# Selective scan on one core: products with C for both channel halves in one GpSimd instruction, in place, and their sums two groups later

## The chip, the core and the metric

The kernel runs on one core of one Trainium2 chip. The metric is the device time of one execution in microseconds; the median of three runs of the kernel before is 34,734.67 us (34,729.47 to 34,738.2). Engines are named as in the profile: PE is TensorE, DVE is VectorE, ACT is ScalarE, POOL is GpSimd, SP issues DMA transfers.

## The reference

Four layers follow each other on an image of 256 x 256 positions with 128 channels. The change touches layer 1 alone, a selective scan in four directions over 256 inner channels with 16 states each:

```python
def selective_scan(xs, dts, As, Bs, Cs, Ds, dt_bias):
    delta = jax.nn.softplus(dts + dt_bias[None, :, :, None])
    ...
    def step(h, inp):
        d_t, x_t, B_t, C_t = inp
        dA = jnp.exp(d_t[..., None] * As)
        h = dA * h + (d_t * x_t)[..., None] * B_t[:, :, None, :]
        y = jnp.einsum('bkdn,bkn->bkd', h, C_t)
        return (h, y)
    ...
    return ys + Ds[None, :, :, None] * xs
```

For every direction k, channel d, state n and position t: h = exp(delta * A) * h + delta * x * B, and y is the sum over the 16 states of h * C. B and C are the same for all channels. Everything is in 32-bit floats.

## The kernel before

The scan stage is the function `scan_stream`. Its four directions are walked one after the other, each in 128 chunks of 512 positions (CH), in all N = 512 chunks. The 256 channels are two halves (dh = 0, 1) of 128 partitions. A chunk is worked in NG = 8 groups, called s = 0 to 7 in its loop: group j handles half j % 2 and the four states that begin at j // 2 * 4. So groups 0 and 1 are the two halves of the same four states and use the same four rows of B and of C; two such groups are called a pair here, numbered 0 to 3 in the chunk.

Each group takes these steps, on four engines:

- `b_product` (L736): the term delta * x * B of 4 states x 512 positions (128 x 2048), on GpSimd for groups 2, 4 and 6, on VectorE for the other five. The table `b_order` says at which s each of them is issued.
- `scans` (L769): two scans of 128 x 1024 on VectorE, each over two states laid end to end. For each, ScalarE first writes the decay exp(delta * A) into one of two PSUM tiles (`l1b_da`, L754, two instructions of 512) and repairs the seam between the two states (L758). The result is `l1b_h`, 4 states x 512.
- `keep_state` (L780): ScalarE copies the last column of h as the start for the next chunk. It is issued in the next group, after the first scan.
- `c_product` (L784): GpSimd multiplies h by C, 128 x 2048, into a tile of its own, `l1b_hc`.
- `sums` (L803): TensorE adds the four states of the product into one of two PSUM tiles `l1b_y`, by four matmuls with the identity. The first group of each half starts the sum with the skip term (L791 or L793, `y_start`). Sums of group g - 2 are issued in group g.
- `y_out` (L813): ScalarE copies the finished sum of a chunk into the output block, at s = 1 and s = 2 of the next chunk.

Between these stands the preparation of the next chunk on TensorE and ScalarE: `dt` (L675) writes delta before its softplus into the PSUM tile `l1b_mm`, `soft_abs` and `soft_exp` (L687 to L695) form the parts of the softplus, `soft_sum` (L701) adds them on TensorE, `delta_copy` (L709) takes the result, `delta_x` (L717, VectorE) multiplies it by x in PSUM, and for half 0 `du_copy` (L725, ScalarE, at s = 4) copies that product to SBUF for GpSimd. `dt` of half 1 comes after it, since it overwrites the same tile. `xproj` (L643, at s = 5) computes dt, B and C of the chunk after next.

The order on each engine is the order in which the Python code issues the instructions (`manual_schedule`); only the waits are derived from the tiles. A tile pool with `bufs=3` gives three buffers in turn: the first write to the fourth tile waits until the last use of the first has ended. `l1b_h` and `l1b_hc` have three buffers of 128 x 2048 each. B and C arrive as broadcasts of 1 MB per pair (`load_b`, L663; `load_c`, L669), three buffers each, issued by SP in the code's order, behind the last use of the buffer that they fill.

Of the kernel before, what the change touches and what calls it, by code (L numbers as in the profile page):

```python
# [10 lines left out]
F32 = mybir.dt.float32  # L11
AF = mybir.ActivationFunctionType
ALU = mybir.AluOpType
# [4 lines left out]
P = 128  # L18
S = 256
NPOS = S * S  # L20
CH = 512
# [530 lines left out]
def scan_stream(c, xc2, y, w):  # L552
# [7 lines left out]
    tc, nc = c.tc, c.nc  # L560
    G, BL, NG = 4, 1024, 8
# [8 lines left out]
    N = len(chunks)  # L570
    with ExitStack() as a:
# [3 lines left out]
        wk = a.enter_context(tc.tile_pool(name="l1b_wk", bufs=2))  # L575
        dram = a.enter_context(tc.tile_pool(name="l1b_dr", bufs=4, space=DRAM))
        ps1 = a.enter_context(tc.tile_pool(name="l1b_p1", bufs=1, space=PSUM))
        states = [st.tile([P, 2, 16], F32, name=f"l1b_state{k}") for k in range(4)]
# [6 lines left out]
        ys = [ps1.tile([P, CH], F32, name=f"l1b_y{dh}") for dh in range(2)]  # L585
# [2 lines left out]

        mm = ps1.tile([P, CH], F32, name="l1b_mm")
        du1 = ps1.tile([P, CH], F32, name="l1b_du")  # L590
        blocks, bcs, bbs, ccs, soft, dls, dbs, hs, hcs = ({} for _ in range(9))

        def cols(ch):
            return bass.ds(chunks[ch][1] * CH % BL, CH)
# [1 line left out]
        def in_block(yo, ch, dh):  # L596

            k, i = chunks[ch]
            if k % 2 == 0:
                return yo[:, dh, cols(ch)]  # L600
            v = yo[:, dh].rearrange("p (b w r) -> p w b r", w=NW, r=R)
            return v[:, bass.ds(i * CH % BL // S, CH // S)]
# [62 lines left out]
        def load_c(m):  # L665
            if m < 4 * N:
                n0 = 16 + m % 4 * G
                cc = ccs[m] = bcp.tile([P, G, CH], F32, name="l1b_cc")
                nc.sync.dma_start(cc, bcs[m // 4][n0 : n0 + G][None].to_broadcast([P, G, CH]))  # L669
# [13 lines left out]
        def soft_abs(ch):  # L683
            if ch >= N:
                return
            soft[ch] = [wk.tile([P, CH], F32, name=f"l1b_{n}", bufs=1) for n in ("tail", "relu")]
            nc.scalar.activation(soft[ch][0], mm, AF.Abs)  # L687
            nc.scalar.activation(soft[ch][1], mm, AF.Relu)

        def soft_exp(ch):  # L690
            if ch >= N:
                return
            tail = soft[ch][0]
            nc.scalar.activation(tail, tail, AF.Exp, scale=-1.0)
            nc.scalar.activation(tail, tail, AF.Ln, bias=1.0)  # L695
# [7 lines left out]
        def delta_copy(ch, dh):  # L703

            if ch >= N:
                return
            k = chunks[ch][0]
            dl = dls[ch, dh] = wk.tile([P, CH], F32, name=f"l1b_dl{dh}")
            nc.scalar.copy(dl, mm)  # L709
            af = dls[ch, dh, "first"] = wk.tile([P, 16], F32, name=f"l1b_af{dh}")  # L710
            t0 = CH - 1 if k >= 2 else 0
            nc.scalar.activation(af, w["A"][:, k, dh], AF.Exp, scale=dl[:, t0 : t0 + 1])
# [8 lines left out]
        def du_copy(ch):  # L721
            if ch >= N:
                return
            dls[ch, "du"] = wk.tile([P, CH], F32, name="l1b_dus")
            nc.scalar.copy(dls[ch, "du"], mm)  # L725
# [12 lines left out]
        def scans(g, extras):  # L738
            ch, j = divmod(g, NG)
            k, dh, n0, rev = chunks[ch][0], j % 2, j // 2 * G, chunks[ch][0] >= 2  # L740
            db = dbs.pop(g).rearrange("p g t -> p (g t)")
            h = hs[g] = wk.tile([P, G, CH], F32, name="l1b_h", bufs=3)
            hf = h.rearrange("p g t -> p (g t)")
            dl, af = dls[ch, dh], dls[ch, dh, "first"]
            mid = CH - 1 if rev else CH
            for i in range(2):
                one, two = n0 + 2 * i + rev, n0 + 2 * i + 1 - rev
                da = das[i].rearrange("p g t -> p (g t)")
                if g == 0 or ch == N // 2 and j == 0:
                    nc.vector.memset(da[:, mid : mid + 1], 0.0)  # L750
                for n in (one, two):
                    o = n % 2 * CH
                    lo, hi = (0, CH) if n == one else (0, CH - 1) if rev else (1, CH)
                    nc.scalar.activation(  # L754
                        da[:, o + lo : o + hi], dl[:, lo:hi], AF.Exp, scale=w["A"][:, k, dh, n : n + 1]
                    )
                first = db[:, 2 * i * CH + mid : 2 * i * CH + mid + 1]
                nc.scalar.activation(  # L758
                    first,
                    states[k][:, dh, two : two + 1],  # L760
                    AF.Identity,
                    scale=af[:, two : two + 1],
                    bias=first,
                )
                sl = slice(2 * i * CH, 2 * i * CH + 2 * CH)
                h_, a_, d_ = hf[:, sl], da, db[:, sl]
                if rev:
                    h_, a_, d_ = h_[:, ::-1], a_[:, ::-1], d_[:, ::-1]
                nc.vector.tensor_tensor_scan(  # L769
                    h_, a_, d_, states[k][:, dh, one : one + 1], ALU.mult, ALU.add  # L770
                )
                if i == 0 and g:
                    keep_state(g - 1)
                for extra in extras[i]:
                    extra()

        def keep_state(g):
            ch, j = divmod(g, NG)
            k, dh, n0 = chunks[ch][0], j % 2, j // 2 * G
            nc.scalar.copy(states[k][:, dh, n0 : n0 + G], hs[g][:, :, 0 if k >= 2 else CH - 1])  # L780

        def c_product(g):
            hc = hcs[g] = wk.tile([P, G, CH], F32, name="l1b_hc", bufs=3)
            nc.gpsimd.tensor_tensor(hc, hs[g], ccs[g // 2], ALU.mult)  # L784
            hs.pop(g - 1, None)

        def y_start(ch, dh):
            k = chunks[ch][0]
# [8 lines left out]
        def sums(g):  # L797
            ch, j = divmod(g, NG)
            if j < 2:
                y_start(ch, j)  # L800
            hc = hcs.pop(g)
            for i in range(G):
                nc.tensor.matmul(  # L803
                    ys[j % 2], c.ident, hc[:, i], start=False, stop=j // 2 * G + i == 15
                )

        def y_out(ch, dh):
            if ch < 0:
                return
            k, i = chunks[ch]  # L810
            yo = blocks[ch][1]
            got = ys[dh] if k % 2 == 0 else ys[dh].rearrange("p (w b r) -> p w b r", b=S // R, r=R)
            nc.scalar.copy(in_block(yo, ch, dh), got)  # L813
            if dh == 1 and ch % 2 == 1:
                block_dma(k, i, yo, True)
# [23 lines left out]
        for ch in range(N):  # L839
            nxt = ch + 1  # L840
            for s in range(NG):
                g = NG * ch + s
                if s == 3 and ch % 2 == 0:
                    load_y(ch + 2)
                if s == 5 and ch % 2 == 1:
                    load_x(ch + 3)
                if s == 4:
                    delta_x(nxt, 0)
                for j in b_order.get(s, ()):
                    b_product(NG * ch + j)  # L850
                extras = [[], []]
                if s == 1:
                    extras[1] = [lambda: soft_abs(nxt), lambda: y_out(ch - 1, 0)]
                if s == 2:
                    extras = [[lambda: soft_exp(nxt)], [lambda: y_out(ch - 1, 1)]]
                if s == 3:
                    extras[1] = [lambda: delta_copy(nxt, 0)]
                if s == 4:
                    extras[0] = [lambda: du_copy(nxt)]
                if s == 5:  # L860
                    extras = [[lambda: soft_abs(nxt)], [lambda: soft_exp(nxt)]]
                if s == 6:
                    extras[1] = [lambda: xd_copy(ch + 2)]
                if s == 7:
                    extras[0] = [lambda: delta_x(nxt, 1), lambda: b_product(g + 2)]
                    extras[1] = [lambda: delta_copy(nxt, 1)]
                if s == 0:
                    dt(nxt, 0)
                scans(g, extras)
                if s == 2:  # L870
                    soft_sum(nxt)
                if s == 4:
                    dt(nxt, 1)
                if s == 5:
                    xproj(ch + 2)
                if s == 6:
                    soft_sum(nxt)
                if g >= 2:
                    sums(g - 2)
                c_product(g)  # L880
                if s % 2 == 1:
                    load_b(g // 2 + 4)
                    load_c(g // 2 + 3)
        keep = N * NG
        sums(keep - 2)
        y_out(N - 1, 0)
        sums(keep - 1)
        y_out(N - 1, 1)


def scan_weights(c, pool):
# [791 lines left out]
```

## Time and profile before

| Part of the profile before | Value |
|---|---|
| Median time | 34,734.67 us |
| Span of the profiled run | 34,733.3 us |
| Mean granted TensorE clock | 0.914 |
| C products (L784), GpSimd | 18,456.6 us in 4096 instructions |
| B products (L736), GpSimd | 6974.1 us in 1536 instructions |
| B products (L736), VectorE, all three rows | 4656.4 us in 2048 instructions, and 1170.8 us in 512 |
| Sums (L803), TensorE | 16,057.6 us in 32,768 records, 639 ns each |
| State copies (L780), ScalarE | 789.3 us in 4095 instructions |
| Copies of delta * x (L725), ScalarE | 300.2 us in 512 instructions, waiting for L736 |

How it is read: a row of the groups gives the busy time of all instructions of one line and shape, the mean of one, and then how long the engine stood idle right before them and which instruction ended that idleness. An idle stretch matters only on an engine whose lateness others feel. The page averages over all layers, so questions on the scan stage are put to stretches of time inside it, and to the timeline, which lists the instructions in order: start, length (of a run of equal instructions together), engine, line, operation, tiles, the number of instructions, and in brackets the idle time ahead with what ended it. One matmul of the code stands as two records.

### The profile page before, as it was taken

The numbers are of one execution on the slowest core, as the hardware profiler recorded it, in microseconds if no ns is written. First come the engines' busy times: TensorE is split into PE (matmuls) and PEld (weight loads), VectorE is DVE, ScalarE is ACT, GpSimd is POOL, SyncE is SP. The second block draws the span as 40 slices with busy tenths as digits, with TensorE's granted clock in tenths as the row PEclk, the third lists the DMA queues.
The fourth block names the chain that finished last, engine by engine and source line by source line (L and its number), as shares of the span: only waits on it lengthen the run. The fifth ranks groups of instructions, "written<-read, shape, count | busy, mean of one in ns | idle before, by whom it ended". The sixth has DMA issues, their size and how long they took to land. (4 is left out here: it accounts for less than half of the span.)

```text
span 34733.3 us, 255526 instructions
## 1 busy us (share of the span) xinstructions
PE 29234.8 (84%) x72564; PEld 12237.5 (35%) x72564; DVE 31351.6 (90%) x24081; ACT 22504.7 (65%) x46445; POOL 26723.0 (77%) x6476
## 2 busy tenths in 40 slices
PE   7999888888888888888888888888888888878888
PEld 2554333333333333333333333333333333334444
DVE  5668899999999999999999999999999999852699
ACT  3665577777777777777777777777777777432476
POOL 2441199999999999999999999999999999510000
PEclk8999999999999999999999999999999999989888
DMA  3114655555555555555555555555555555674111
GB/s 135 45 45 103 155 190 191 190 191 191 189 192 189 191 191 190 191 190 191 197 200 203 200 201 202 200 201 202 200 203 202 200 202 200 217 197 139 67 34 33
DMA packets 2561382, 5947.79 MB, mean 171 GB/s; under 512 B 899079, under 2 KB 1835800, under 8 KB 1984086
## 3 DMA queue, kind: packets, MB, share of 16 engines
q1 hardware_dynamic: 2424790, 5864.31, 47.3%
q10 hardware_dynamic: 135168, 67.13, 0.6%
q8 instruction: 572, 9.37, 0.1%
q14 instruction: 852, 6.98, 0.1%
HBM read 5238.41 MB, written 692.58 MB: 171 GB/s over the span
## 5 line engine op out<-in xcount | busy, mean ns | idle before, releaser
L769 DVE TENSOR_TENSOR_SCAN l1b_h<-l1b_da,l1b_state,l1b_db 128x1024 f32<-128x1024 f32 x8192 | 18788.8, 2335 | 597.7 <-ACT l1b_db L758 586.6
L784 POOL TENSOR_TENSOR l1b_hc<-l1b_h,l1b_cc 128x2048 f32<-128x2048 f32 x4096 | 18456.6, 4533 | 322.5 <-DVE l1b_h L769 321.7
L803 PE MATMUL l1b_y<-l1b_hc,ident 128*128 128x512 f32 x32768 | 16057.6, 639 | 1124.1 <-POOL l1b_hc L784 1124.0
L754 ACT ACTIVATE l1b_da<-l1b_dl,l_A 128x512 f32<-128x512 f32 (+1 forms) x16384 | 11296.7, 689 | 3153.2 <-DVE l1b_h L769 2845.3
L803 PEld LDWEIGHTS l1b_y<-l1b_hc,ident 128*128 128x128 f32 x32768 | 6526.7, 205 | 10695.3 <-issue 8153.0
L736 POOL TENSOR_TENSOR l1b_db<-l1b_bb,l1b_dus 128x2048 f32<-128x2048 f32 x1536 | 6974.1, 4540 | 1244.8 <-DMA l1b_bb<-l1b_bc 1244.8
L736 DVE TENSOR_TENSOR l1b_db<-l1b_bb,l1b_du 128x2048 f32<-128x2048 f32 x2048 | 4656.4, 2274 | 35.1
L758 ACT ACTIVATE l1b_db<-l1b_state,l1b_db,l1b_af 128x1 f32<-128x1 f32 x8192 | 3045.1, 372 | 0.0
L675 PE MATMUL l1b_mm<-l1b_xd,l_dtw 41*128 41x512 f32 x2048 | 1370.9, 754 | 1698.9 <-ACT l1b_dus L725 1693.2
L701 PE MATMUL l1b_mm<-l1b_tail,ident 128*128 128x512 f32 x2048 | 1295.4, 719 | 1384.3 <-ACT l1b_tail L695 1384.3
L780 ACT COPY l1b_state<-l1b_h 128x4 f32<-128x4 f32 x4095 | 789.3, 193 | 2433.0 <-DVE l1b_h L769 2432.9
L326 POOL TENSOR_TENSOR l0b_e<-l0b_e,l0b_den 128x1024 f32<-128x1024 f32 x512 | 970.0, 1895 | 1402.3 <-DVE l0b_den L325 784.0
L701 PE MATMUL l1b_mm<-l1b_relu,ident 128*128 128x512 f32 x2048 | 1310.3, 728 | 0.0
L675 PEld LDWEIGHTS l1b_mm<-l1b_xd,l_dtw 41*128 41x128 f32 x2048 | 337.3, 206 | 2513.3 <-ACT l1b_dus L725 2116.2
L725 ACT COPY l1b_dus<-l1b_mm 128x512 f32<-128x512 f32 x512 | 300.2, 586 | 1387.5 <-DVE l1b_db L736 1387.0
L736 DVE TENSOR_TENSOR l1b_db<-l1b_bb,l1b_mm 128x2048 f32<-128x2048 f32 x512 | 1170.8, 2287 | 18.2 <-ACT l1b_dus L725 0.7
L302 DVE CUSTOM_DVE_ANT_0 l0b_e<-l0b_sc,l0b_bias 128x256 f32<-128x256 f32 x2048 | 745.5, 421 | 419.3 <-PE l0b_sc L291 415.9
L701 PEld LDWEIGHTS l1b_mm<-l1b_tail,ident 128*128 128x128 f32 x2048 | 377.6, 207 | 2055.0 <-ACT l1b_tail L695 1810.6
L493 DVE SCALAR_TENSOR_TENSOR l1a_mm<-l1a_xi,l1a_each,l1a_mm 128x512 f32<-128x512 f32 x1408 | 1046.0, 755 | 59.0 <-issue 12.9
L643 PE MATMUL l1b_du<-l1b_xc,l_xproj 128*40 128x512 f32 x2048 | 981.5, 602 | 62.5 <-DMA l_xproj<-in_l_xproj 58.6
L317 ACT ACTIVATE l0b_e<-l0b_e,l0b_top 128x256 f32<-128x256 f32 x2048 | 1012.0, 498 | 1.9 <-DVE l0b_top L302 1.9
L709 ACT COPY l1b_dl<-l1b_mm 128x512 f32<-128x512 f32 x1024 | 588.3, 574 | 524.1 <-DVE l1b_du L717 516.6
(256 smaller groups left out, 28736.5 us busy)
## 6 DMA issues: line engine op xcount, KB each, us to landing
l1b_bb<-l1b_bc SPq DMA_DIRECT2D x2048, 1024.0 KB
l1b_cc<-l1b_bc SPq DMA_DIRECT2D x2048, 1024.0 KB
l1b_xc<-l_xc SPq DMA_DIRECT2D x128, 1024.0 KB
l_y<-l1b_yo SPq DMA_DIRECT2D x128, 1024.0 KB
l1b_xc<-l_xct SPq DMA_DIRECT2D x128, 1024.0 KB
l_y<-l1b_yo SPq DMA_DIRECT2D x256, 512.0 KB
l_xc<-l1a_o SPq DMA_DIRECT2D x64, 1024.0 KB
l_xct<-l1a_ot SPq DMA_DIRECT2D x16, 4096.0 KB
```

What stands on the lines that cost most here:

```text
L317: nc.scalar.activation(e[:, i], e[:, i], AF.Exp, scale=-1.0, bias=top[:, i : i + 1], accum_out=den[:, i : i + 1],)
L326: nc.gpsimd.tensor_tensor(e, e, den[:, :, None].to_broadcast([P, 4, S]), ALU.mult)
L493: nc.vector.scalar_tensor_tensor(mm, xis[i][:, r + dy : r + dy + 2, dx : dx + S], each[:, dh, tap : tap + 1], mm, ALU.mult, ALU.add,)
L643: nc.tensor.matmul(du1[:40], w["xproj"][:, dh, k, :], blocks[ch][0][:, dh, cols(ch)], start=dh == 0, stop=dh == 1,)
L675: nc.tensor.matmul(mm, w["dt"][:, chunks[ch][0], dh * P : dh * P + P], xds[ch % 3][0:41], start=True, stop=True,)
L701: nc.tensor.matmul(mm, c.ident, part, start=i == 0, stop=i == 1)
L736: eng.tensor_tensor(db, bbs[g // 2], du[:, None, :].to_broadcast([P, G, CH]), ALU.mult)
L754: nc.scalar.activation(da[:, o + lo : o + hi], dl[:, lo:hi], AF.Exp, scale=w["A"][:, k, dh, n : n + 1])
L758: nc.scalar.activation(first, states[k][:, dh, two : two + 1], AF.Identity, scale=af[:, two : two + 1], bias=first,)
L769: nc.vector.tensor_tensor_scan(h_, a_, d_, states[k][:, dh, one : one + 1], ALU.mult, ALU.add)
L784: nc.gpsimd.tensor_tensor(hc, hs[g], ccs[g // 2], ALU.mult)
L803: nc.tensor.matmul(ys[j % 2], c.ident, hc[:, i], start=False, stop=j // 2 * G + i == 15)
```

## The change

The two halves of a pair now share one tile `l1b_h` of 2 x 4 x 512 per partition, in three buffers, and `l1b_hc` is gone. The scans write the halves; once both are scanned, a single GpSimd instruction of 4096 elements per partition multiplies the whole tile by C in place, C being broadcast over the halves. It is issued after the scans of the following group, at even s. The sums read `l1b_h` and come in group g for group g - 4 instead of g - 2, so that `y_out` moves from s = 1 and 2 to s = 3 and 4, and the `y_start` that opens a chunk's sums moves from s = 2 and 3 to s = 4 and 5. The loads of C and of the x and y blocks move to fit. The aim is fewer GpSimd instructions and hand-overs, in the same amount of memory.

```diff
@@ scans
-            h = hs[g] = wk.tile([P, G, CH], F32, name="l1b_h", bufs=3)
-            hf = h.rearrange("p g t -> p (g t)")
+            if j % 2 == 0:
+                hs[g // 2] = wk.tile([P, 2, G, CH], F32, name="l1b_h", bufs=3)
+            hf = hs[g // 2][:, j % 2].rearrange("p g t -> p (g t)")
@@ keep_state, c_product
-            nc.scalar.copy(states[k][:, dh, n0 : n0 + G], hs[g][:, :, 0 if k >= 2 else CH - 1])
-
-        def c_product(g):
-            hc = hcs[g] = wk.tile([P, G, CH], F32, name="l1b_hc", bufs=3)
-            nc.gpsimd.tensor_tensor(hc, hs[g], ccs[g // 2], ALU.mult)
-            hs.pop(g - 1, None)
+            last = 0 if k >= 2 else CH - 1
+            nc.scalar.copy(states[k][:, dh, n0 : n0 + G], hs[g // 2][:, j % 2, :, last])
+
+        def c_product(m):
+
+            h = hs[m]
+            nc.gpsimd.tensor_tensor(h, h, ccs[m][:, None].to_broadcast([P, 2, G, CH]), ALU.mult)
@@ sums
-            hc = hcs.pop(g)
             for i in range(G):
                 nc.tensor.matmul(
-                    ys[j % 2], c.ident, hc[:, i], start=False, stop=j // 2 * G + i == 15
+                    ys[j % 2], c.ident, hs[g // 2][:, j % 2, i], start=False, stop=j // 2 * G + i == 15
                 )
+            if j % 2:
+                del hs[g // 2]
@@ the loop over chunks and groups
-                if s == 3 and ch % 2 == 0:
+                if s == 5 and ch % 2 == 0:
                     load_y(ch + 2)
-                if s == 5 and ch % 2 == 1:
+                if s == 6 and ch % 2 == 1:
                     load_x(ch + 3)
...
                 if s == 1:
-                    extras[1] = [lambda: soft_abs(nxt), lambda: y_out(ch - 1, 0)]
+                    extras[1] = [lambda: soft_abs(nxt)]
                 if s == 2:
-                    extras = [[lambda: soft_exp(nxt)], [lambda: y_out(ch - 1, 1)]]
+                    extras[0] = [lambda: soft_exp(nxt)]
                 if s == 3:
-                    extras[1] = [lambda: delta_copy(nxt, 0)]
+                    extras[1] = [lambda: delta_copy(nxt, 0), lambda: y_out(ch - 1, 0)]
                 if s == 4:
-                    extras[0] = [lambda: du_copy(nxt)]
+                    extras = [[lambda: du_copy(nxt)], [lambda: y_out(ch - 1, 1)]]
...
-                if g >= 2:
-                    sums(g - 2)
-                c_product(g)
+                if g >= 4:
+                    sums(g - 4)
+                if s % 2 == 0 and g >= 2:
+                    c_product(g // 2 - 1)
+                    load_c(g // 2 + 2)
                 if s % 2 == 1:
                     load_b(g // 2 + 4)
-                    load_c(g // 2 + 3)
```

After the last chunk the last product, four sums and two output copies follow.

More of the change, by code (lines that the diff above doesn't have):

```diff
@@ L590, in scan_stream @@
         du1 = ps1.tile([P, CH], F32, name="l1b_du")
-        blocks, bcs, bbs, ccs, soft, dls, dbs, hs, hcs = ({} for _ in range(9))
+        blocks, bcs, bbs, ccs, soft, dls, dbs, hs = ({} for _ in range(8))
         def cols(ch):
@@ L877, in scan_stream @@
                     soft_sum(nxt)
-                if g >= 2:
-                    sums(g - 2)
-                c_product(g)
+                if g >= 4:
[3 more added lines that the diff above has]
+                    load_c(g // 2 + 2)
                 if s % 2 == 1:
                     load_b(g // 2 + 4)
-                    load_c(g // 2 + 3)
[L884 to L888, printed above, removed]
+        c_product(N * NG // 2 - 1)
+        for j in range(4):
+            sums(N * NG - 4 + j)
+        for dh in range(2):
+            y_out(N - 1, dh)
 def scan_weights(c, pool):
```

## The prediction

> **What bounds the kernel now.** I read the page first (engine shares, then the costliest groups), then the groups of a window of 1000 us, then the timeline of a single chunk.
>
> ```profile
> PE 29234.8 (84%) x72564; PEld 12237.5 (35%) x72564; DVE 31351.6 (90%) x24081; ACT 22504.7 (65%) x46445; POOL 26723.0 (77%) x6476
> ...
> L769 DVE TENSOR_TENSOR_SCAN l1b_h<-l1b_da,l1b_state,l1b_db 128x1024 f32<-128x1024 f32 x8192 | 18788.8, 2335 | 597.7 <-ACT l1b_db L758 586.6
> L784 POOL TENSOR_TENSOR l1b_hc<-l1b_h,l1b_cc 128x2048 f32<-128x2048 f32 x4096 | 18456.6, 4533 | 322.5 <-DVE l1b_h L769 321.7
> ```
>
> The scan stage runs 512 chunks of 8 groups: 8192 scans are 16 per chunk, 4096 products with C are 8. In a window of 1000 us inside it VectorE is busy 974.9 us and GpSimd 987.8, and windows in all four scan directions agree within 0.4%. So both engines are nearly full. The waits say which one drives: VectorE waits for ScalarE (L758), GpSimd waits for VectorE's scans (L769). VectorE together with a short ScalarE burst is the pace. Its idle time is 597.7 / 512 = 1.17 us per chunk, all that a removed wait could give back.
>
> One chunk in the timeline (s is the group within the chunk). VectorE:
>
> ```profile
> 15038.83 2.29 DVE L736 TENSOR_TENSOR l1b_db<-l1b_bb,l1b_mm 128x2048 f32<-128x2048 f32 x1
> 15041.03 6.95 DVE L769 TENSOR_TENSOR_SCAN l1b_h<-l1b_da,l1b_state,l1b_db 128x1024 f32<-128x1024 f32 x3
> 15048.61 2.35 DVE L769 TENSOR_TENSOR_SCAN l1b_h<-l1b_da,l1b_state,l1b_db 128x1024 f32<-128x1024 f32 x1 [0.62 <-ACT l1b_db L758]
> 15051.47 6.83 DVE L769 TENSOR_TENSOR_SCAN l1b_h<-l1b_da,l1b_state,l1b_db 128x1024 f32<-128x1024 f32 x3 [0.52 <-ACT l1b_db L758]
> ```
>
> The two idle stretches (0.62 and 0.52 us) are the whole loss of the chunk; the second scan of s=5 stands at 15048.61, the first scan of s=6 at 15051.47. The same start came at 15001.53 one chunk earlier: the period is 49.94 us. ScalarE and TensorE in the same stretch:
>
> ```profile
> 15041.15 0.59 ACT L725 COPY l1b_dus<-l1b_mm 128x512 f32<-128x512 f32 x1 [2.71 <-DVE l1b_db L736]
> ...
> 15041.79 1.12 PE L675 MATMUL l1b_mm<-l1b_xd,l_dtw 41*128 41x512 f32 x2 [3.06 <-ACT l1b_dus L725]
> 15042.84 5.40 PE L803 MATMUL l1b_y<-l1b_hc,ident 128*128 128x512 f32 x8
> 15048.17 1.91 PE L643 MATMUL l1b_du<-l1b_xc,l_xproj 128*40 128x512 f32 x4
> 15050.01 3.70 PE L803 MATMUL l1b_y<-l1b_hc,ident 128*128 128x512 f32 x8
> 15053.55 1.02 PE L701 MATMUL l1b_mm<-l1b_tail,ident 128*128 128x512 f32 x2
> ```
>
> This chain matters below. At s=4 the B product of the next chunk must end before ScalarE may copy l1b_mm (L725); only then may TensorE compute the next dt (L675), and everything behind that in TensorE's order stands: one group's sums (8 records, two per matmul), xproj (4), another group's sums. They end about 15053.6. In this kernel no scan waits for them: L784 writes a tile of its own, so l1b_h is free once GpSimd has read it.
>
> **What the Trainium skill says.** "GPSIMD Engine Reference", section "Elementwise — side-by-side cycle accounting": a two-input tensor_tensor costs about 2.6 cycles per element, measured 4497 ns at 2048 elements. The trace agrees (4533), and back-to-back pairs last 9.01 to 9.05 us here, so one instruction of 4096 should take about 9.0. "TensorE: Matmul & The Clock Gate", section "Part 1: The HAM clock gate": after idling for about one window of 3.4 us TensorE runs at half clock until it has been busy for about as long. The trace agrees: after the 3.06 us gap some records come 0.85 us apart instead of 0.43. "SBUF — State Buffer", section "Who interferes with whom": a VectorE instruction with at most one SBUF input, outside its 2-port modes, does not contend with GpSimd. The scan reads da from PSUM and the B product reads its du from PSUM, so I expect neither engine to slow or relieve the other.
>
> **The change part by part.**
>
> *Products.* 4096 x 4533 ns becomes 2048 x about 9.0 us: per chunk 4 x 9.03 + 3 x 4.54 = 49.7 us, as now. If the fixed cost of 4 instructions (60 to 100 ns each, an estimate from 4497 ns against 2.6 cycles x 2048 at the page's 1.2 GHz) went, 0.2 to 0.4 us would be saved, on an engine that is not the pace. Unknown: in place, with C broadcast over the halves. In-place rows of the page are 128x1024 in 1895 ns (L326, 1.85 ns per element, 7.6 us for 4096) and 128x512 in 1563 ns (L961, 3.05, 12.5 us). I take 9.0 because pattern and stage match; both ends go to the rivals. Each product now waits for the last group's state copy (L780), which runs within 0.2 us of the scan's end, and GpSimd has other work queued ahead.
>
> *Transfers.* C loads wait for the product three pairs back. Placing the new products in the frame above (previous pair 3 at 15013.6 to 15022.6, then B product, pair 0 from 15027.1 to 15036.1, B product, pair 1 from 15040.6 to 15049.6) C loads go out at 22.6, 36.1, 49.6, 63.1, with the B load behind each. The tightest is the B load at 22.9, needed at 38.83: the DMA view moves the 2 MB of both at about 420 GB/s, 5 us. Nothing is exposed.
>
> *y_out at s=3 and s=4.* The same 0.57 us copies. At s=3 ScalarE sits idle 1.95 us before the next exponentials, and at s=4 it idles 0.64 us at 15045.78. At most 0.1 us each.
>
> *The new wait.* l1b_h now lives until the sums have read it, in 3 buffers of two groups. In the built order, the first scan of each even group carries a wait for TensorE's last sums matmul three pairs back. Resolving which one: s=0 waits for sums(3), s=2 for sums(5), s=4 for the previous sums(7), and **s=6 for sums(1) of the same chunk**. The first three have room of 2 us and more. sums(1) has not: in TensorE's order it comes after dt at s=4, the y start for half 0, sums(0), xproj and the y start for half 1. Behind the waiting scan stand all of VectorE's work, hence ScalarE (das buffers) and GpSimd.
>
> The chain, counted from the start of the B product at 15038.83: dt starts +2.96. From dt to the second group of sums: in 27 chunks that I looked at it was 8.2 us (10 of them), 9.4 to 9.9 (15) or 6.5 (2, warm throughout). The timeline above is one of the 8.2 us. Before dt TensorE will have been idle for 3.2 to 5.3 us instead of 3.1 to 4.1, so rather colder: I take 9.2. The two y starts, which move into this chain, add 4 records x 0.43 = 1.71. sums(1) itself runs 3.54 to the next start; hand-over 0.1 (an estimate: 0.05 us lie between ScalarE's end and dt's start). Sum 2.96 + 9.2 + 1.71 + 3.54 + 0.1 = 17.51. The scan of s=6 starts now at 51.47 - 38.83 = 12.64. **Added: 4.87 us per chunk.** ScalarE's two stalls lie inside the 12.64 and are counted already. The next chunk can't win it back: du copy, dt and sums hang on VectorE's progress at s=4, so the wait returns each time. 512 x 4.87 = 2493 us; 34,735 + 2,493 = **37,228 us**. GpSimd (49.7 us) has room in a period of 54.8.
>
> *The end* of the stage: the last pair's product and four sums run after the last scan, some 9 + 15 us once. Negligible.
>
> **Rivals.**
>
> A. *Faster.* The wait at s=6 is met in time and VectorE loses its ScalarE stalls: at most 598 + 35 us of idle, 34,100. For it: GpSimd is 98.8% busy and gets fewer instructions. Against: the chain above ends after 15053.6 today, before anything is added to it, and the ScalarE work that makes the stall is unchanged. 0.06; unchanged within 0.2%: 0.02.
>
> B. *TensorE warm.* Chain 6.5 instead of 9.2: 2.17 us per chunk, 35,850. Against: the gap before dt grows. 0.06.
>
> C. *GpSimd the bound.* At 3.05 ns per element the product takes 12.5 us, a chunk 4 x 12.5 + 13.6 = 63.6, +13.7 us, 41,750. Against: 512-element rows carry more fixed cost per element. Up to 10.2 us per product it would still hide under 54.8. 0.07.
>
> D. *The forecast.* 0.79. With the chain at 8.2: 3.87 us, 36,716; at 9.9: 5.57, 37,587; if half clock lasted a little longer still, 5.9, 37,750. An early B or du copy by some tenths gives the low end 36,400. A, B and C lie outside this range with 0.21 in all. Faster 0.06, same 0.02, slower 0.92.
>
> **What would show it.** Right: the scans' row has about 2900 us of idle time before it, most put down to TensorE's sums and not to L758; the period is near 54.8 us; VectorE's busy share in the stage falls to about 89%, GpSimd's to 91%; the product's row has 2048 of about 9.0 us; the timeline shows the first scan of s=6 starting just behind the second sums after xproj. Wrong: a scan row still waiting on L758 alone (A); sums ending near 53.6 in this frame (B); a product of 10 us and more, with scans or sums waiting for GpSimd (C).

## The result, and the profile after

The changed kernel takes 37,137.55 us (median of 4 runs, 37,129.77 to 37,142.44) against 34,732.77 us before on the same chip (also the median of 4 runs): a ratio of 1.0692, with a 95% interval of 1.0673 to 1.0711. Per chunk that is (37,137.55 - 34,732.77) / 512 = 4.70 us more. The forecast was 37,228 us, 4.87 us per chunk, with a range of 36,400 to 37,750.

The page after the change: the engines' busy time, then three of the costliest groups.

```profile
PE 29059.6 (78%) x72564; PEld 12297.0 (33%) x72564; DVE 31352.5 (84%) x24081; ACT 22503.0 (61%) x46445; POOL 26402.5 (71%) x4428
...
L770 DVE TENSOR_TENSOR_SCAN l1b_h<-l1b_da,l1b_state,l1b_db 128x1024 f32<-128x1024 f32 x8192 | 18792.5, 2336 | 2990.7 <-PE l1b_y L804 2657.1
L787 POOL TENSOR_TENSOR l1b_h<-l1b_h,l1b_cc 128x4096 f32<-128x4096 f32 x2048 | 18146.2, 8860 | 3037.8 <-ACT l1b_state L782 3037.8
L804 PE MATMUL l1b_y<-l1b_h,ident 128*128 128x512 f32 x32768 | 14784.1, 602 | 12.3 <-POOL l1b_h L787 12.2
```

VectorE is busy for the same time as before (31,352.5 us against 31,351.6), and its scans have the same length (2336 ns against 2335). What grew is the idle time before the scans, from 597.7 to 2990.7 us, that is by 2393 us of the 2395 us by which the span grew. Most of it, 2657.1 us, now ends with TensorE's sums (L804); before, nearly all of it ended with ScalarE. GpSimd does its products in less time than before (18,146 us against 18,457) and then stands idle for 3038 us: the engine that the change relieves got faster, and nothing came of it. TensorE, whose sums the scans wait for, is itself busy for only 78% of the span. It is late at one place, not full.

The timeline of one chunk after, VectorE:

```profile
15017.25 2.29 DVE L736 TENSOR_TENSOR l1b_db<-l1b_bb,l1b_mm 128x2048 f32<-128x2048 f32 x1
15019.46 6.95 DVE L770 TENSOR_TENSOR_SCAN l1b_h<-l1b_da,l1b_state,l1b_db 128x1024 f32<-128x1024 f32 x3
15027.03 2.35 DVE L770 TENSOR_TENSOR_SCAN l1b_h<-l1b_da,l1b_state,l1b_db 128x1024 f32<-128x1024 f32 x1 [0.62 <-ACT l1b_db L759]
15034.57 6.83 DVE L770 TENSOR_TENSOR_SCAN l1b_h<-l1b_da,l1b_state,l1b_db 128x1024 f32<-128x1024 f32 x3 [5.18 <-PE l1b_y L804]
```

and TensorE beside it:

```profile
15020.22 2.07 PE L675 MATMUL l1b_mm<-l1b_xd,l_dtw 41*128 41x512 f32 x2 [5.14 <-ACT l1b_dus L725]
15022.22 2.08 PE L795 MATMUL l1b_y<-l1b_xc,l_dsum 128*128 128x512 f32 x2
15024.09 4.04 PE L804 MATMUL l1b_y<-l1b_h,ident 128*128 128x512 f32 x8
15028.06 1.91 PE L643 MATMUL l1b_du<-l1b_xc,l_xproj 128*40 128x512 f32 x4
15029.90 1.12 PE L795 MATMUL l1b_y<-l1b_xc,l_dsum 128*128 128x512 f32 x2
15030.86 3.60 PE L804 MATMUL l1b_y<-l1b_h,ident 128*128 128x512 f32 x8
15034.30 1.02 PE L701 MATMUL l1b_mm<-l1b_tail,ident 128*128 128x512 f32 x2
```

The first scan of s=6 has one idle stretch of 5.18 us, where 0.52 us stood before, and it starts just behind the second sums after xproj, which are sums(1). TensorE waited 5.14 us for the copy of L725 before it could begin dt, and sums(0) stood behind dt in its order, although its input lay ready: pair 0's product had ended on GpSimd at 15014.45. The same stall came at 15089.18, a period of 54.61 us.

### The profile page after: what moved, and what is told of

Read it like the earlier page. It is cut to its first block, busy times and chain, and to the rows that moved or that the text cites. A ratio compares the mean times of both kernels' runs of the same rounds, so it can differ in the third digit from the quotient of the medians.

```text
span 37128.0 us, 248050 instructions
## 1 busy us (share of the span) xinstructions
PE 29059.6 (78%) x72564; PEld 12297.0 (33%) x72564; DVE 31352.5 (84%) x24081; ACT 22503.0 (61%) x46445; POOL 26402.5 (71%) x4428
## 4 chain that ended last, share of the span: by engine, by line
DVE 43%; PE 29%; ACT 12%; issue 6%; DMA 1%; SPq 0%; DVEq 0%; another core or an unknown queue 0%; POOL 0%; ACTq 0%; POOLq 0%
DVE l1b_h L770 26%; DVE l1b_db L736 12%; PE l1b_y L804 10%; ACT l1b_da L755 5%; PE l1b_mm L675 3%; PE l1b_du L643 3%; PE l1b_y L795 2%; PE l1b_y L793 2%; ACT l1b_db L759 1%; PE l2f_fp L1276 1%; DVE l1a_mm L493 1%; PE l2f_op L1283 1%; PE l1a_mm L479 1%; DVE l1b_du L717 1%; DVE l1b_mm L717 1%
## 5 line engine op out<-in xcount | busy, mean ns | idle before, releaser
L770 DVE TENSOR_TENSOR_SCAN l1b_h<-l1b_da,l1b_state,l1b_db 128x1024 f32<-128x1024 f32 x8192 | 18792.5, 2336 | 2990.7 <-PE l1b_y L804 2657.1
L787 POOL TENSOR_TENSOR l1b_h<-l1b_h,l1b_cc 128x4096 f32<-128x4096 f32 x2048 | 18146.2, 8860 | 3037.8 <-ACT l1b_state L782 3037.8
L804 PE MATMUL l1b_y<-l1b_h,ident 128*128 128x512 f32 x32768 | 14784.1, 602 | 12.3 <-POOL l1b_h L787 12.2
L804 PEld LDWEIGHTS l1b_y<-l1b_h,ident 128*128 128x128 f32 x32768 | 6430.5, 197 | 8650.9 <-issue 8511.0
L736 POOL TENSOR_TENSOR l1b_db<-l1b_bb,l1b_dus 128x2048 f32<-128x2048 f32 x1536 | 6956.6, 4529 | 1245.5 <-DMA l1b_bb<-l1b_bc 1245.5
L701 PE MATMUL l1b_mm<-l1b_tail,ident 128*128 128x512 f32 x2048 | 1585.9, 867 | 4134.3 <-ACT l1b_tail L695 4134.3
L675 PE MATMUL l1b_mm<-l1b_xd,l_dtw 41*128 41x512 f32 x2048 | 1635.0, 889 | 2632.2 <-ACT l1b_dus L725 2626.5
L701 PE MATMUL l1b_mm<-l1b_relu,ident 128*128 128x512 f32 x2048 | 1419.0, 785 | 0.0
L725 ACT COPY l1b_dus<-l1b_mm 128x512 f32<-128x512 f32 x512 | 300.1, 586 | 1388.4 <-DVE l1b_db L736 1388.0
L479 PE MATMUL l1a_mm<-l1a_xp,l1a_taps 128*128 128x512 f32 x1792 | 851.5, 617 | 73.3 <-ACT l1a_ot L512 73.3
```

The costliest lines, as they stand in the source:

```text
L479: nc.tensor.matmul(mm, taps[:, tap, dh * P : dh * P + P], xps[b][:, r + dy : r + dy + 2, dx : dx + S], start=n == 0, stop=n == len(on_pe[u ...
L675: nc.tensor.matmul(mm, w["dt"][:, chunks[ch][0], dh * P : dh * P + P], xds[ch % 3][0:41], start=True, stop=True,)
L701: nc.tensor.matmul(mm, c.ident, part, start=i == 0, stop=i == 1)
L736: eng.tensor_tensor(db, bbs[g // 2], du[:, None, :].to_broadcast([P, G, CH]), ALU.mult)
L770: nc.vector.tensor_tensor_scan(h_, a_, d_, states[k][:, dh, one : one + 1], ALU.mult, ALU.add)
L787: nc.gpsimd.tensor_tensor(h, h, ccs[m][:, None].to_broadcast([P, 2, G, CH]), ALU.mult)
```

## Experiments

### 1. Sums one group earlier

```diff
-                if g >= 4:
-                    sums(g - 4)
+                if g >= 3:
+                    sums(g - 3)
...
-        for j in range(4):
-            sums(N * NG - 4 + j)
+        for j in range(3):
+            sums(N * NG - 3 + j)
```

> The changed kernel with one thing different: sums come in group g for group g - 3 instead of g - 4, so that sums(0) stands ahead of dt at s=4 and sums(1) right behind it, with xproj after both. Theory (the buffer wait): the first scan of s=6 waits for sums(1), which hangs behind dt, two y starts, sums(0) and xproj. Now sums(1) ends about 7 us earlier, near 49 us in the frame in which the scan can start at 51.5, so the wait goes and the period falls from 54.6 to about 49.9 us: 34,700 to 34,800 us. Rival (the product itself, in place and over 4096 elements, slows the scans or GpSimd): the product is the same, so the time stays near 37,100. Rival (ScalarE's y_out copies at s=3 and 4 cost time): they are the same too, 37,100.

Measured: 34,705.92 us, ratio to the kernel before 0.9992 (0.9983 to 1.0). The scans' row on its page:

```profile
L770 DVE TENSOR_TENSOR_SCAN l1b_h<-l1b_da,l1b_state,l1b_db 128x1024 f32<-128x1024 f32 x8192 | 18792.2, 2336 | 560.6 <-ACT l1b_db L759 550.0
```

The product is the same instruction in the same tile, the y_out copies stand at the same groups, and the whole loss is gone. The idle time is back at the kernel before's size and with its releaser. So neither the in-place product of 4096 elements nor y_out cost anything that shows; the place of the sums in TensorE's order did. It also shows that the change's own aim, fewer GpSimd instructions, moves the time by no more than the measurement can tell while VectorE sets the pace.

### 2. A fourth buffer, the late sums kept

```diff
-        bcp = a.enter_context(tc.tile_pool(name="l1b_bc", bufs=3))
+        bcp = a.enter_context(tc.tile_pool(name="l1b_bc", bufs=2))
...
-                hs[g // 2] = wk.tile([P, 2, G, CH], F32, name="l1b_h", bufs=3)
+                hs[g // 2] = wk.tile([P, 2, G, CH], F32, name="l1b_h", bufs=4)
...
+                if s in (0, 2, 4):
+                    load_b(g // 2 + 3)
                 if s % 2 == 0 and g >= 2:
                     c_product(g // 2 - 1)
-                    load_c(g // 2 + 2)
-                if s % 2 == 1:
-                    load_b(g // 2 + 4)
+                    load_c(g // 2 + 1)
+                if s == 7:
+                    load_b(g // 2 + 3)
```

The loads ahead of the loop are two pairs instead of three, to match.

> The changed kernel with four buffers of l1b_h instead of three; room for them is made by two buffers of B and two of C instead of three, with their loads issued at other groups. The order of TensorE is unchanged, sums at g - 4. Theory (the buffer wait): the first scan of s=6 now waits for the sums of the pair four back, which ended in the chunk before; the period falls to 49.9 us and the time to 34,700 to 34,800, perhaps 100 more if a B load lands late. Rival (TensorE's later order costs time by another way than the buffer, for instance through dt or soft_sum): the order is the same, so the time stays near 37,100.

Measured: 34,858.47 us, 1.0035 (1.0021 to 1.0049). TensorE keeps its order, and in the timeline its stretch from dt to sums(1) is about as long as in the changed kernel (10.0 to 11.8 us in 60 chunks); no scan in those 60 chunks, 3000 us of the run, waits for it. That sets the buffer apart from the order: **sums(1) is just as late, but nothing needs its buffer.** The 122 us that remain against the kernel before are 0.24 us per chunk. VectorE's waits within 1000 us of this run show a term of that size:

```profile
DVE l1b_h L770 <- ACT l1b_db L759: 21.3, 40, 0.6
DVE l1b_du L717 <- PE l1b_mm L701: 4.7, 8, 0.7
```

The first line is ScalarE's burst. The second is new: soft_sum comes right behind the late sums(1), so VectorE's delta_x of s=7 sometimes waits for it: 4.7 us in 20 chunks, 0.24 us each. Between 5000 and 30,000 us of the run these waits sum up to 114.7 us, nearly all of what remains. The smaller number of B buffers is a rival for it: GpSimd's B products waited 1636.4 us for transfers in this run against 1245.5 in the changed kernel. But no wait of VectorE in the scan stage is put down to a transfer or to GpSimd.

### 3 and 4. TensorE kept busy ahead of dt

```diff
                 if s == 4:
+                    for _ in range(2):
+                        xproj(ch + 2)
                     dt(nxt, 1)
```

> The changed kernel with more work for TensorE: xproj of the chunk after next is computed two more times (8 records, about 3.8 us), just ahead of dt at s=4, where TensorE stood idle 5.14 us. Theory (half clock is a term of the chain): TensorE arrives at dt warm, the chain from dt to sums(1) shrinks from 8.9 + 1.7 to about 6.5 + 1.7 us, the added time per chunk from 4.70 to about 2.3 us: 35,900 us, and the TensorE records in that stretch are 0.43 us apart. Rival (the clock isn't the term, the chain is long by its number of matmuls): the time stays near 37,140 or gets longer.

Measured: 36,516.54 us, 1.0512 (1.0496 to 1.0527). It is faster than the changed kernel although TensorE does more, which the rival excluded, but 617 us slower than expected. In 56 chunks the stretch from dt to the second sums took 8.3 or 8.4 us in 20 and 10.0 or 10.1 in 36; the stall before s=6 was 2.9 us in 20 and 4.6 to 5.0 in 36. One of the slow ones, TensorE:

```profile
15039.92 3.63 PE L643 MATMUL l1b_du<-l1b_xc,l_xproj 128*40 128x512 f32 x8
15045.18 1.12 PE L675 MATMUL l1b_mm<-l1b_xd,l_dtw 41*128 41x512 f32 x2 [1.64 <-ACT l1b_dus L725]
15046.24 1.94 PE L795 MATMUL l1b_y<-l1b_xc,l_dsum 128*128 128x512 f32 x2
15047.97 4.53 PE L804 MATMUL l1b_y<-l1b_h,ident 128*128 128x512 f32 x8
```

The two y start records take 1.94 us (at full clock 1.13, as in the next run), after a gap of only 1.64 us. So the gap was closed once more, with a third repetition (`range(3)`).

> As the run with xproj computed two more times ahead of dt at s=4, but three more times (12 records, about 5.5 us), so that TensorE has no gap left there. With two, the stretch from dt to sums(1) took 8.3 us in a third of the chunks and 10.0 in the others, after a gap of 1.3 to 1.6 us. Theory (half clock after idle time is the term): without a gap nearly all chunks take 8.3 us; dt itself comes about 0.3 us later, so about 2.4 + 0.3 = 2.7 us are added per chunk to the kernel before: 36,100 us. Rival (half clock comes from the long gap earlier in the chunk, ahead of soft_sum, or by chance): the share of chunks at 10.0 us stays, and the time is that of two repeats plus 0.3 us per chunk, 36,670.

Measured: 36,250.78 us, 1.0437 (1.0419 to 1.0454). Now the stretch took 8.3 or 8.4 us in all 56 chunks of the same 3000 us:

```profile
15096.29 5.34 PE L643 MATMUL l1b_du<-l1b_xc,l_xproj 128*40 128x512 f32 x12
15101.57 1.12 PE L675 MATMUL l1b_mm<-l1b_xd,l_dtw 41*128 41x512 f32 x2
15102.62 1.13 PE L795 MATMUL l1b_y<-l1b_xc,l_dsum 128*128 128x512 f32 x2
15103.58 3.60 PE L804 MATMUL l1b_y<-l1b_h,ident 128*128 128x512 f32 x8
```

Half clock is thus a term of the chain, worth 10.68 - 8.35 = 2.3 us per chunk in the changed kernel (means of 55 and 56 chunks). The time is 150 us above the expectation. The stall alternates between 2.9 us (27 of 57) and 4.0 us (28): in the second kind the sums ahead of the repeated xproj run slow (7.99 us for 16 records where the first kind has 7.03), after TensorE's other gap of 8 us ahead of soft_sum. dt then starts 1.1 us later. The rival, the long gap earlier in the chunk, is right for that part only.

### 5. xproj behind sums(1)

```diff
-                if s == 5:
-                    xproj(ch + 2)
...
                     sums(g - 4)
+                if s == 5:
+                    xproj(ch + 2)
```

> The changed kernel with one move: at s=5 TensorE does sums(1) first and xproj after it. Nothing is added or removed. Theory (the chain ends with sums(1) and everything ahead of it in TensorE's order counts): the chain is shorter by xproj's 1.84 us, so 4.70 - 1.84 = 2.86 us are added per chunk: 36,200 us. Rival (the scan waits for something else that ends at the same time): 37,140.

Measured: 36,542.39 us, 1.052 (1.0504 to 1.0535), 3.53 us per chunk instead of 4.70. Direction and cause hold, the size is 1.17 us where 1.84 was expected. The stretch from dt to sums(1) fell from 10.68 to 9.51 us (means of 55 and 56 chunks), the same 1.17. Without half clock it would be 8.35 - 1.84 = 6.5 (an estimate), so half clock costs 3.0 us here against 2.3. The clock record of the traces agrees: from dt to the end of sums(1) the granted clock was half for 6.55 us per chunk here and for 4.88 us in the changed kernel (means of the same chunks). The move made TensorE's slow phase longer and gave part of its gain back.

### 6 and 7. Versions without either wait

The wait that is left, VectorE for ScalarE, can be covered with other work: the B product of group 7 goes to the group in which ScalarE has its burst. First in the kernel before:

```diff
-    b_order = {0: (3,), 1: (4,), 2: (5,), 3: (6, 7), 4: (8,), 6: (10,)}
+    b_order = {0: (3,), 1: (4,), 2: (5,), 3: (6,), 4: (8,), 5: (7,), 6: (10,)}
```

> The kernel before with one move: VectorE's B product of group 7 is issued at s=5 instead of s=3, so that it stands where ScalarE has its burst of softplus work. Theory: the two waits of VectorE for ScalarE (1.17 us per chunk) go, and GpSimd with 11 instructions per chunk (8 x 4.49 + 3 x 4.49 = 49.4 us) becomes the pace: period 49.4 instead of 49.93 us, 34,460 us. Rival (ScalarE's waits return elsewhere): unchanged, 34,740.

Measured: 34,409.11 us, 0.9908 (0.9893 to 0.9923). A stretch of 1000 us of this run:

```profile
core 0: us, PE busy (x) PEld busy (x) DVE busy (x) ACT busy (x) POOL busy (x), PEclk, DMA share, GB/s
12000.00:13000.00 1000.00, 818.51 (x1702) 319.52 (x1701) 984.04 (x468) 713.34 (x1456) 1000.00 (x224) 0.94 0.52 193
```

and the scans' row of its page:

```profile
L769 DVE TENSOR_TENSOR_SCAN l1b_h<-l1b_da,l1b_state,l1b_db 128x1024 f32<-128x1024 f32 x8192 | 18732.8, 2334 | 385.2 <-ACT l1b_db L758 331.4
```

GpSimd has no idle time left: it is the bound, as expected. The theory had VectorE's waits for ScalarE go as well, but 331.4 us of 586.6 are left. They stand elsewhere now, some 40 us behind the B product of s=4, and in the timeline at 20010.05 such a wait follows ScalarE's own wait of 2.70 us for the sums ahead of `y_out`. These sums come from GpSimd's products, so VectorE is probably held back by GpSimd along this way. Then the same move on top of experiment 1:

> The changed kernel with sums in group g for group g - 3, and VectorE's B product of group 7 issued at s=5 instead of s=3. Theory: neither the buffer wait nor ScalarE's waits are left; GpSimd needs 4 x 8.82 + 3 x 4.5 = 48.8 us per chunk, VectorE 48.8: period about 49.0 us, 34,260 us, some 200 us less than the kernel before with the same move, which is what the joined products are worth once GpSimd sets the pace. Rival (joining the products is worth nothing even then): the same time as that kernel.

Measured: **34,135.71 us, 0.9828 (0.9814 to 0.9843)**, the fastest version here. On its page:

```profile
L770 DVE TENSOR_TENSOR_SCAN l1b_h<-l1b_da,l1b_state,l1b_db 128x1024 f32<-128x1024 f32 x8192 | 18677.8, 2331 | 16.1 <-ACT l1b_db L759 5.4
L787 POOL TENSOR_TENSOR l1b_h<-l1b_h,l1b_cc 128x4096 f32<-128x4096 f32 x2048 | 18444.1, 9069 | 23.7 <-ACT l1b_state L782 21.3
```

VectorE's waits for ScalarE are gone, and GpSimd again has no idle time. Against the kernel before with the same move it is 273 us faster (some 200 were expected), 0.53 us per chunk. That is what the joined products and their layout are worth, and it shows only where GpSimd sets the pace. How it comes about can be read from the starts on GpSimd, first experiment 6, then 7:

```profile
14996.29 13.47 POOL L784 TENSOR_TENSOR l1b_hc<-l1b_h,l1b_cc 128x2048 f32<-128x2048 f32 x3
15009.73 4.52 POOL L736 TENSOR_TENSOR l1b_db<-l1b_bb,l1b_dus 128x2048 f32<-128x2048 f32 x1
...
15002.05 9.22 POOL L787 TENSOR_TENSOR l1b_h<-l1b_h,l1b_cc 128x4096 f32<-128x4096 f32 x1
15010.87 4.88 POOL L736 TENSOR_TENSOR l1b_db<-l1b_bb,l1b_dus 128x2048 f32<-128x2048 f32 x1
```

The records of a GpSimd that never idles overlap (9.22 us long, but 8.82 to the next start), so starts are the better measure. A product of 2048 elements takes (15009.73 - 14996.29) / 3 = 4.48 us, one of 4096 takes 8.82. A pair saves 2 x 4.48 - 8.82 = 0.14 us, four pairs 0.56 us per chunk, and nearly all of it is had. With three B products of 4.49 us GpSimd needs 4 x 8.82 + 3 x 4.49 = 48.75 us per chunk, and the mean period of this run is 48.76: GpSimd still sets the pace.

## Why the prediction was right

**The wait.** Named as the first scan of s=6 behind sums(1) of the same chunk; the timeline after shows it there, and experiments 1 and 2 remove the time by taking away either the lateness or the need for the buffer.

**The sum, term by term**, from the start of the B product at 15017.25. dt starts after 2.97 us (2.96 predicted). From dt to sums(1) with both y starts it is 10.64 us (9.2 + 1.71 = 10.91). sums(1) takes 3.44 us (3.54). The hand-over to VectorE is 0.27 us (0.1). Together 17.32 us against 17.51, since the errors partly cancel, and 4.70 us added per chunk against 4.87.

**The choice of 9.2 us** between the two clusters of before was the uncertain step. It landed close, but the mixture behind it did not appear: 50 of 55 chunks took 10.6 or 10.7 us, so in the terms of before about 8.9 to 9.0 us nearly every time. The direction of my argument, colder because of a longer gap, gave 0.3 us too much. That it came so close is in part luck: the prediction did not foresee that all chunks would behave alike, for which the last section gives a likely reason, and for either cluster alone its own figures are 3.87 and 5.57 us.

**Work put at nothing.** ScalarE's y_out at s=4 fell into its idle time before the next state copy, which shrank from 0.64 to 0.32 us, and the 0.62 us stall at s=5 kept its size. GpSimd's wait for B transfers was 1244.8 us and is 1245.5; in both kernels nearly all of that is one wait ahead of GpSimd's first B product of the stage, so within the stage the moved loads exposed nothing. The product cost 8.86 us where I took 9.0, which is off the path in this kernel.

**Rivals.** A needs the sums in time: experiment 1 makes them so and gives 0.9992, since ScalarE's stalls stay; they went only in experiment 7, where work was put beside them as well. B, the warm chain, doesn't happen by itself, but its term is real (experiment 4). C falls with the 8.86 us. The Trainium skill's 2.6 cycles per element ("GPSIMD Engine Reference", section "Elementwise — side-by-side cycle accounting") give 8.87 us for 4096 elements at the page's 1.2 GHz, as an estimate, and the trace agrees (8.86).

## What to carry to other kernels

Before a product is written in place, ask who reads the tile last: the buffer then lives until the slowest reader is done, and in an engine with a fixed order that reader stands behind everything issued ahead of it, here a matmul that in the end waits for VectorE itself. Find the last reader that the first write waits for and add up the order in front of it. Relieving an engine that doesn't set the pace bought nothing by itself; with the sums one group earlier, and once GpSimd had become the pace-setter, the same edit was worth 0.8%.

## What the runs showed of the hardware

Work added to TensorE made the kernel faster by 2.4% (36,250.78 against 37,137.55 us), because matmuls on an idle engine kept its clock up for a chain that waited (mean granted clock 0.915 instead of 0.882); even a matmul of 40 output rows served.

The traces record the granted clock itself. In all nine it has two values, full and half, and its changes fall on one grid of 3.413 us, within 0.03 us. What matters is how a gap lies in this grid. Two chunks of experiment 3 show it: for each, the grid step with the gap ahead of dt (1.09 us in the first, 1.64 in the second), and the step behind it. The granted clock is the third figure from the end:

```profile
core 0: us, PE busy (x) PEld busy (x) DVE busy (x) ACT busy (x) POOL busy (x), PEclk, DMA share, GB/s
14991.81:14995.21 3.40, 2.34 (x5) 0.97 (x6) 3.38 (x3) 2.94 (x6) 3.40 (x1) 1.00 0.97 286
14995.23:14998.62 3.39, 3.39 (x9) 1.29 (x8) 3.39 (x2) 3.03 (x7) 3.39 (x1) 1.00 0.74 228
15043.01:15046.41 3.40, 1.76 (x5) 0.47 (x4) 3.40 (x2) 1.83 (x4) 3.40 (x2) 1.00 0.83 345
15046.43:15049.82 3.39, 3.39 (x5) 1.33 (x5) 3.37 (x3) 3.03 (x9) 3.39 (x1) 0.50 0.02 5
```

With TensorE busy for 2.34 us of a step the clock stayed, with 1.76 us the next step ran at half clock. In this run the two kinds of chunk are cleanly apart (463 chunks between 4300 and 29,000 us): the clock stayed full in all 162 chunks with a gap up to 1.14 us and fell in all 301 with 1.15 us or more. That is shorter than the idle window of about 3.4 us that the Trainium skill names ("TensorE: Matmul & The Clock Gate", section "Part 1: The HAM clock gate"). The longer gap of 8 us earlier in each chunk does not separate the two: it is the same in both, and before the fall at 15046.42 the clock had been full again for 13.65 us.

In the changed kernel nearly every period is 54.61 or 54.62 us, which is 16 times 3.413 us, the length of the page's free-running window. The same four stretches of clock come back in 434 of some 439 chunks, half for two steps, full for nine, half for two, full for three; the first begins at 15018.15, just ahead of dt:

```profile
15018.20:15024.90 6.70, 4.68 (x5) 1.68 (x6) 6.68 (x4) 4.93 (x11) 6.70 (x2) 0.50 1.02 317
15025.10:15055.60 30.50, 26.06 (x60) 10.26 (x58) 24.66 (x13) 18.45 (x39) 24.57 (x4) 1.00 0.40 142
15055.80:15062.40 6.60, 3.19 (x4) 1.51 (x5) 6.60 (x4) 4.98 (x11) 6.60 (x2) 0.50 0.75 315
```

Two other kernels that wait for TensorE's chain do this over more than one chunk: with three repetitions of xproj two chunks take 105.81 us, 31 steps, and with xproj behind sums(1) three chunks take 160.43 us, 47 steps. In these three runs 95% of the cases or more lie within 0.05 us of the whole number. The kernel before, whose pace does not hang on TensorE, has 49.94 us, 14.63 steps. So the chunk locks onto the grid. A likely reason is that a stall which ends with the return of the clock sets each chunk back onto the grid; no run tested that alone. Experiment 3 with two repetitions is not locked (160.33 us for three chunks, 46.97 steps), and there half clock costs the chain either nothing or one whole step, wherever dt stands in the grid.
